# A two-layer graph network on one core: the last graph's final head gets its own finishing steps, and the validity check moves into the issue order

## The chip, the cores and the metric

One Trainium2 chip, one of its cores. The metric is the device time of one run in microseconds, the median of three runs. Before the change it is 1749.58 us (1746.99 to 1750.99).

## The reference

Sixteen graphs of 1024 nodes with 256 features each, and a 1024 x 1024 integer adjacency that is symmetric, holds 0 or 1 and has ones on its diagonal. Two layers follow each other, each with a residual and a layer norm.

```python
# layer 0: gated sum over neighbours
e0 = leaky(einsum('bid,bjd->bij', h * a0[:, 0], h))     # e1..e3 for adj == 2, 3, 4
alpha = sigmoid(where(adj == 1, e0, neg_inf))
x = layernorm(x + einsum('bij,bjd->bid', alpha, h) + bias)
# layer 1: attention, H = 4 heads of F = 64
Wh = (X @ W).reshape(B, N, H, F)
e = leaky_relu(e_src[:, :, None, :] + e_dst[:, None, :, :], 0.2)
alpha = softmax(where(A > 0, e, -1e9), axis=2)
x = layernorm(x + elu(einsum('bijh,bjhf->bihf', alpha, Wh)).reshape(B, N, H * F))
```

## The kernel before

Everything of a graph stays on the core: its nodes are 8 row blocks of 128 (`NB`), which form two halves of four blocks (`NH`, `NQ`); a half has two *pairs* of blocks. The function `stages` builds some 60 named generators for a graph, each a list of steps with `yield` between them. A table gives every step a due time: `FIRST` for graph 0, `LAST` for graph 15, `TIMES` for the 14 between, with 112 of table time between graphs. `issue` (before: L1136 and on) sorts all steps of all graphs by due time and emits them. The tables thus set nothing but the order of instructions on each engine; an engine takes its instructions in that order and waits for its inputs at each of them. Steps of neighbouring graphs lie between each other: while one graph does its attention, the next does its gates. The last graph has no next one, so its attention runs alone at the end.

What the stages near the end of a graph do, for each of the four heads `h` and the two halves:

- `pos` (VectorE, L646): for one head, one half and one of 8 source blocks, the masked comparison that tells on which side of the leaky slope an edge lies; 128x512. 64 of them in a graph.
- `acc` (TensorE, L658): the product of that mask with the head's factors; it needs the `pos` tile. `acc_low` (ScalarE, L673) and `acc_sum` (VectorE, L681) add its two halves of precision into `u`, 128x2x130 for one head of one pair.
- `weigh`: for the second half first `ts - u` on VectorE (L758, 128x520 for four heads), then a product with `rho` (`times`, L746), which in the last two graphs is eight ScalarE instructions of 128x65, one for each of 2 rows and 4 heads.
- `divide`: VectorE adds the two parts (L768, 128x512), forms the denominator (L771) and its reciprocal (L773), and `times` multiplies by it (eight ScalarE instructions of 128x64).
- `elu` (ScalarE Exp, L793, 128x512) and `join` (two VectorE instructions, L785 and L787, 128x512) give the activation and add it to the residual `y`.
- `moments1`, `gathered1` (VectorE, L432 and L438), `spread1` (GpSimd, L456 and L457), `shift1` (VectorE, L465) and `norm1` (L475 on VectorE, L477 on ScalarE) are the layer norm; `leave` (L802) sends the rows out, for the last half in two transfers, and its last step takes the running maximum of the reciprocals (`zinv`, L804).

All of `weigh`, `divide`, `elu` and `join` handle a pair with all four heads at once, so for the second half they can begin only when the last head's `acc` has been summed.

The fast path holds only for adjacencies of zeros and ones that are symmetric and for scores of bounded size. After `issue` comes a check of the whole batch (L1316 to L1337): the sums of adjacency and mask (`more`, through a TensorE product `pmore`), the largest score (`span`), the largest reciprocal (`zinv`), three comparisons, a transpose on TensorE (`pm`), a minimum (`good`) and `flag`. This part lies outside the order written out by hand; the framework's own scheduler placed it, and its early pieces stand earlier in the stream. Then every engine loads `flag` (L1339) and branches over a general path that isn't taken here (L1342).

At the start of the kernel, `setup` loads small weights through SyncE's queue and multiplies them on VectorE (L237, L239); `turn`, `mask` and `cast` bring the adjacency in, `score`, `leak`, `leaky`, `sigmoid`, `below`, `lower`, `upper`, `self_loop` make the gate, `agg` sums over the neighbours.

Of the kernel before, what the change touches and what calls it, by code (L numbers as in the profile page):

```python
# [27 lines left out]
P = 128  # L28
# [168 lines left out]
def stages(nc, k, pl, b, xg, adjg, outg, sums, span, zinv):  # L197
# [516 lines left out]
    def parts(half, pair):  # L714

        u = t["u", half, pair]
        return u[..., 0:F], u[..., F : 2 * F], u[..., 2 * F], u[..., 2 * F + 1]

    def second(half, pair):

        return t["u", half, pair][..., F : 2 * F + 1]

# [18 lines left out]
    def times(val, by):  # L741

        if late:
            for q in range(2):
                for h in range(H):
                    nc.scalar.activation(  # L746
                        val[:, q, h, :], val[:, q, h, :], AF.Copy, scale=by[:, q, h : h + 1]
                    )
        else:
            by = by.unsqueeze(3).to_broadcast(list(val.shape))  # L750
            nc.vector.tensor_tensor(val, val, by, ALU.mult)

    def weigh():
        for half, pair in PAIRS:
            ib = half * NQ + 2 * pair
            u2 = second(half, pair)
            if half:
                nc.vector.tensor_tensor(u2, t["ts", pair][..., 0 : F + 1], u2, ALU.subtract)  # L758
                yield
            times(u2, t["rho"][:, ib : ib + 2])  # L760
            yield

    def divide():
        t["rz"] = small("rzs", NB, H)
        for half, pair in PAIRS:
            ib = half * NQ + 2 * pair
            o, u2, z2, z1 = parts(half, pair)
            nc.vector.tensor_tensor(o, o, u2, ALU.add)  # L768
            yield
            rz = t["rz"][:, ib : ib + 2]  # L770
# [8 lines left out]
    def join():  # L779
        for half, pair in PAIRS:  # L780
            o, ex, _, _ = parts(half, pair)
            yp = t["y", half][:, 2 * pair : 2 * pair + 2, :].rearrange(
                "p q (h f) -> p q h f", h=H
            )
            nc.vector.scalar_tensor_tensor(o, o, 0.0, yp, ALU.max, ALU.add)  # L785
            yield
            nc.vector.scalar_tensor_tensor(yp, ex, 1.0, o, ALU.min, ALU.add)  # L787
            yield

    def elu():  # L790
        for half, pair in PAIRS:
            o, ex, _, _ = parts(half, pair)
            nc.scalar.activation(ex, o, AF.Exp)  # L793
            yield

    def leave():
        for half in range(NH):
# [5 lines left out]
            if half == NH - 1:  # L803
                nc.vector.tensor_tensor(zinv, zinv, t["rz"], ALU.max)  # L804
            yield

# [11 lines left out]
        weigh=weigh(), divide=divide(), elu=elu(), join=join(),  # L818
        moments1=moments("1"), gathered1=gathered("1"),
        spread1=spread("1"), shift1=shift("1"), norm1=norm("1"), leave=leave(),  # L820
    )

# [104 lines left out]
    "leave": [206.44, 240.93],  # L927
}
FIRST = {
    "aload": [-145.70, -145.40, -144.40, -143.60, -141.20, -140.10],  # L930
    "cast": [-146.10, -145.60, -144.60, -143.90, -142.60, -142.00, -140.90, -139.50],
    "turn": [-145.90, -145.10, -144.50, -143.20, -142.30, -141.30, -140.30, -139.30],
    "mask": [-145.30, -144.90, -143.80, -142.80, -141.70, -141.10, -139.40, -139.10],
    "setup": [-142.90, -140.70, -138.30],
    "xt": [-147.20, -147.10, -147.00, -146.80],
    "xtc": [-146.90, -146.70, -146.60, -146.40],
    "xta": [-146.50, -145.80, -144.20, -142.20, -141.80, -139.90, -139.60, -137.00],
    "score": [
        -146.20, -145.50, -144.80, -144.70, -143.40, -143.10, -142.10, -141.50, -140.40,
        -138.90, -138.60, -136.60,  # L940
    ],
    "leak": [
        -145.20, -144.30, -144.10, -144.00, -143.00, -142.70, -141.60, -141.40, -139.70,
        -138.50, -137.70, -136.40,
    ],
    "leaky": [
        -145.00, -143.70, -143.50, -143.30, -142.40, -141.90, -141.00, -140.60, -139.20,
        -137.90, -137.30, -135.60,
    ],
    "sigmoid": [-142.50, -140.80, -138.20, -137.10, -136.10, -135.00, -133.50, -132.80],  # L950
    "below": [
        -140.50, -140.20, -138.80, -138.00, -137.50, -136.80, -135.70, -135.20, -134.30,
        -132.70,
    ],
    "lower": [
        -140.00, -139.80, -138.40, -136.70, -136.00, -135.90, -134.90, -134.70, -133.40,
        -131.90,
    ],
    "upper": [-139.00, -137.60, -136.50, -135.10, -134.20, -133.00, -132.30, -131.80],
    "self_loop": [-138.70, -137.40, -135.50, -134.60, -133.80, -132.50, -131.60, -131.20],  # L960
    "agg": [
        -138.10, -137.80, -137.20, -136.20, -135.30, -134.80, -134.50, -133.90, -133.60,
        -133.20, -132.60, -132.40, -132.10, -131.40, -131.30, -130.60,
    ],
    "residual": [-136.90, -134.40, -133.70, -133.30, -133.10, -132.00, -130.90, -130.20],
    "moments0": [-135.80, -134.10, -132.90, -132.20, -131.10, -130.70, -130.40, -130.10],
    "gathered0": [-135.40, -134.00, -131.70, -131.50, -130.50, -130.30, -96.07, 17.17],
    "spread0": [-131.00, 20.28],
    "shift0": [-130.80, 24.26],
    "norm0": [6.67, 11.00, 11.41, 12.51, 25.36, 25.99, 26.71, 27.01],  # L970
    "yt": [17.15, 19.47, 29.04, 29.13],
    "ytc": [19.36, 19.69, 29.17, 29.53],
    "project": [20.27, 22.38, 25.24, 26.22, 32.78, 40.85, 41.12, 41.80],
    "wh": [25.15, 27.94, 28.22, 36.80, 41.06, 42.84, 42.85, 44.25],
    "sources": [43.57, 44.67],
    "rows": [44.50, 47.17],
    "keep_rows": [46.30, 54.62],
    "top_dve": [46.04, 47.34, 49.10, 49.48, 50.03],
    "top_pe": [46.11, 49.26],
    "exps": [51.13],  # L980
    "product": [51.24, 51.61, 51.65, 55.99, 64.09, 71.97, 73.66, 74.28],
    "high": [54.44, 56.34, 58.73, 61.00, 69.95, 72.79, 74.04, 74.66],
    "low": [54.68, 57.50, 65.30, 66.50, 71.75, 77.68, 77.72, 77.72],
    "sload": [50.22, 76.32, 79.88, 84.60, 99.79, 115.99, 126.87, 141.84],
    "pos": [
        56.38, 56.65, 59.61, 60.83, 61.90, 62.47, 66.98, 72.25, 78.79, 79.58, 80.30,
        81.29, 81.91, 83.89, 85.64, 86.24, 94.25, 94.83, 97.97, 99.15, 100.99, 101.36,
        101.95, 101.97, 105.63, 106.23, 106.73, 107.47, 108.82, 109.31, 109.42, 109.44,
        111.05, 111.90, 112.37, 114.78, 114.79, 114.81, 115.82, 117.22, 117.23, 120.53,
        122.14, 122.30, 123.00, 123.69, 124.94, 127.40, 128.22, 130.84, 132.75, 133.15,  # L990
        134.26, 137.15, 140.15, 141.06, 143.44, 144.05, 145.63, 146.94, 153.65, 154.27,
        155.46, 159.89,
    ],
    "acc": [
        61.10, 61.65, 61.72, 63.59, 69.81, 72.90, 74.47, 75.10, 81.40, 83.30, 83.92,
        84.50, 84.62, 86.15, 88.72, 89.34, 98.53, 98.69, 100.90, 100.97, 102.11, 102.79,
        105.80, 106.18, 108.03, 108.18, 108.25, 109.02, 109.72, 109.72, 110.35, 110.44,
        113.56, 114.38, 116.31, 117.04, 117.43, 119.10, 119.20, 119.89, 122.26, 122.73,
        122.79, 124.03, 124.41, 124.82, 125.15, 127.73, 134.85, 139.77, 140.29, 142.76,
# [388 lines left out]
```

## Time and profile before

| | before |
|---|---|
| median of three runs | 1749.58 us |
| profiled execution, its own time | 1748.92 us |
| its span in the trace | 1747.1 us |
| TensorE busy | 1695.6 us (97%) |
| VectorE busy | 1639.0 us (94%) |
| ScalarE busy | 1237.6 us (71%) |
| granted TensorE clock | 0.99 |

Between 120 and 1550 us TensorE is busy for 1429.49 of 1430.00 us. The stretches that matter here are the first 120 us and those from 1550 us on. ScalarE's two activation tables, one with Sigmoid and one with Exp, replace each other: 87 table loads of 1283 ns on the fast path.

### The profile page before, as it was taken

The page shows a single profiled execution, that of the slowest core. Times are in us where ns is not written, and L with a number is a line of the kernel's source. Part 1 is how long each engine was busy: PE and PEld are TensorE (multiplying, and loading weights), DVE is VectorE, ACT ScalarE, POOL GpSimd, SP SyncE. Part 2 cuts the span into 40 slices and gives each one's busy share as a digit, 9 for nine tenths or more (in the row PEclk, how much of TensorE's full clock was granted, in tenths as well). Part 3 has the DMA queues.
Part 4 walks back from the last instruction along what each step waited for, and adds up shares of the span by engine and source line. Part 5 has one row for each costly group of instructions (what it writes and reads, how often), then busy time and mean ns, then how long its engine had stood idle before and what let it go on. Part 6 is the DMA issues. An engine that isn't in the chain of part 4 may idle for free.

```text
span 1747.1 us, 29629 instructions
## 1 busy us (share of the span) xinstructions
PE 1695.6 (97%) x10579; PEld 1494.8 (86%) x10579; DVE 1639.0 (94%) x3640; ACT 1237.6 (71%) x2770; POOL 107.1 (6%) x138
## 2 busy tenths in 40 slices
PE   7999999999999999999999999999999999999884
PEld 4789898998979889898998989889898998979883
DVE  4498999999999999999999999999999999999997
ACT  6673967759587685967759586685957769585675
POOL 0001000010000101000010000101000010000100
PEclk9999999999999999999999999999999999999987
DMA  5452343434334343343434334343342435331020
GB/s 184 109 127 75 93 109 88 109 91 129 90 90 101 109 119 91 98 98 91 109 93 135 81 98 108 99 115 91 97 110 78 109 74 139 79 74 49 26 67 26
DMA packets 249274, 168.60 MB, mean 97 GB/s; under 512 B 133280, under 2 KB 232736, under 8 KB 249120
## 3 DMA queue, kind: packets, MB, share of 16 engines
q1 hardware_dynamic: 249120, 166.63, 36.3%
q8 instruction: 86, 1.41, 0.3%
q14 instruction: 68, 0.56, 0.1%
HBM read 118.10 MB, written 17.04 MB: 77 GB/s over the span
## 4 chain that ended last, share of the span: by engine, by line
PE 83%; issue 7%; DVE 4%; ACT 3%; DMA 1%; POOL 0%; SPq 0%; POOLq 0%; ACTq 0%; DVEq 0%
PE agg L415 24%; PE acc L658 24%; PE tot L701 13%; PE e L344 11%; PE pw L505 6%; PE pg L383 2%; DVE pos L646 1%; PE pt L308 1%; PE pt L486 1%; DMA sbc<-sdram 1%; DMA aT<-a 0%; ACT mT L295 0%; ACT a L273 0%; DVE gm L628 0%; DVE gate L364 0%
## 5 line engine op out<-in xcount | busy, mean ns | idle before, releaser
L646 DVE SCALAR_TENSOR_TENSOR pos<-sbc,nd,mT 128x512 fp32r<-128x512 f32 x1024 | 732.0, 738 | 7.6 <-DMA sbc<-sdram 4.5
L658 PE MATMUL acc<-gm,pos 128*128 128x260 f32 x4096 | 613.3, 293 | 6.5 <-DVE u L681 2.8
L658 PEld LDWEIGHTS acc<-gm,pos 128*128 128x128 f32 x4096 | 538.7, 190 | 19.5 <-issue 3.8
L415 PE MATMUL agg<-xb,gate 128*128 128x256 f32 x2048 | 463.3, 379 | 0.0
L415 PEld LDWEIGHTS agg<-xb,gate 128*128 128x128 f32 x2048 | 380.0, 190 | 46.9 <-DVE gate L407 0.6
L701 PE MATMUL tot<-gm,allm 128*128 128x264 f32 x2048 | 328.4, 297 | 7.1 <-ACT gm L621 5.0
L701 PEld LDWEIGHTS tot<-gm,allm 128*128 128x128 f32 x2048 | 281.1, 190 | 11.7 <-ACT gm L621 5.2
L344 PE MATMUL e<-xT,xTa 128*128 128x512 f32 (+3 forms) x768 | 265.6, 490 | 3.1 <-ACT xTa L332 1.6
L344 PEld LDWEIGHTS e<-xT,xTa 128*128 128x128 f32 x768 | 135.3, 191 | 106.9 <-issue 53.4
L673 ACT COPY low<-acc 128x260 f32<-128x260 f32 x256 | 89.9, 377 | 190.3 <-PE acc L658 190.3
L693 ACT CAST allm<-mT 128x512 fp32r<-128x512 uint8 x256 | 157.5, 616 | 27.9 <-PE tot L701 26.6
L477 ACT ACTIVATE y<-y,shift,rstd 128x256 f32<-128x256 f32 x254 | 136.8, 591 | 41.8 <-DVE shift L465 41.8
L273 ACT ACTIVATE a<-a 128x1024 bf16<-128x1024 int32 x128 | 135.6, 1060 | 41.0 <-DMA aT<-a 19.3
L295 ACT ACTIVATE mT<-aT 128x1024 uint8<-128x1024 bf16 x120 | 127.2, 1060 | 6.4 <-DMA aT<-a 6.3
L456 POOL TENSOR_SCALAR std<-mv 128x4 f32<-128x4 f32 x64 | 27.0, 421 | 1626.0 <-DVE mv L438 1426.5
L364 DVE TENSOR_TENSOR gate<-e,gate 128x512 f32<-128x512 f32 x192 | 104.2, 550 | 21.3 <-ACT gate L356 21.2
L505 PE MATMUL pw<-w_aug,yT 128*128 128x264 f32 x512 | 122.2, 387 | 0.7 <-ACT yT L495 0.6
L681 DVE TENSOR_TENSOR u<-acc,low 128x260 f32<-128x260 f32 x256 | 102.1, 419 | 16.6 <-ACT low L673 16.6
L432 DVE BATCH_NORM_STATS2 st<-y 128x6 f32<-128x256 f32 x256 | 105.8, 415 | 1.2
L505 PEld LDWEIGHTS pw<-w_aug,yT 128*128 128x128 f32 x512 | 93.4, 190 | 15.6 <-ACT yT L495 1.7
L356 ACT ACTIVATE gate<-e 128x512 f32<-128x512 f32 x192 | 90.0, 486 | 14.6 <-PE e L344 14.5
L400 DVE TENSOR_TENSOR gate<-gate,mT 128x1024 f32<-128x1024 f32 (+7 forms) x128 | 95.8, 748 | 4.5 <-PE pg L383 2.4
(97 smaller groups left out, 1775.9 us busy)
## 6 DMA issues: line engine op xcount, KB each, us to landing
a<-in_adj_dram SPq DMA_DIRECT2D x128, 512.0 KB, 4.7
sbc<-sdram SPq DMA_DIRECT2D x128, 256.0 KB, 4.6
out_dram<-y SPq DMA_DIRECT2D x31, 512.0 KB, 3.5
xb<-in_x_dram SPq DMA_DIRECT2D x15, 1024.0 KB, 5.2
aT<-a SPq DMA_TRANSPOSE x120, 3.1
xb<-in_x_dram SPq DMA_DIRECT2D x2, 512.0 KB, 4.2
sdram<-srow SPq DMA_DIRECT2D x32, 8.0 KB, 1.4
out_dram<-y SPq DMA_DIRECT2D x2, 256.0 KB, 2.3
```

Source lines behind the costliest of these rows:

```text
L273: nc.scalar.activation(t["a16", ib], t["a32", ib], AF.Copy, accum_out=sums[:, 0, at : at + 1])
L295: nc.scalar.activation(t["mT"][:, :, ib * P : (ib + 1) * P], t["aT", ib], AF.Square, accum_out=sums[:, 1, at : at + 1],)
L344: nc.tensor.matmul(e[:, 0:n], lhsT=t["xTa", jb][:, c, :], rhs=t["xT"][:, c, at : at + n], start=(c == 0), stop=(c == DC - 1),)
L364: nc.vector.tensor_tensor(ge, t["e", jb, at][:, 0:n], ge, ALU.max)
L415: nc.tensor.matmul(agg[:, 0:D], lhsT=t["gate"][:, jb, ib * P : (ib + 1) * P], rhs=t["xb"][:, jb, :], start=(jb == 0), stop=(jb == NB - 1),)
L432: nc.vector.bn_stats(st, t["y", half][:, q, :])
L477: nc.scalar.activation(y, y, AF.Identity, bias=shift, scale=rstd)
L505: nc.tensor.matmul(pw[:, 0:WD], lhsT=t["yT"][:, c, jb * P : (jb + 1) * P], rhs=k.w_aug[:, c, :], start=(c == 0), stop=(c == DC - 1),)
L646: nc.vector.scalar_tensor_tensor(p_, t["sbc", half, h], t["nd"][:, jb, h : h + 1], t["mT"][:, jb, half * HALF : (half + 1) * HALF], ALU.is ...
L658: nc.tensor.matmul(t["acc", half, h, q // 2][:, q % 2, 0 : 2 * E], lhsT=t["pos", half, h, jb][:, q * P : (q + 1) * P], rhs=pl.gm[:, h, jb] ...
L693: nc.scalar.copy(m_, t["mT"][:, j0 : j0 + 4, ib * P : (ib + 1) * P])
L701: nc.tensor.matmul(tot[:, 0 : H * F1], lhsT=t["allm", ib, jb // 4 * 4][:, jb % 4, :], rhs=pl.gm[:, :, jb, l, F:E], start=(jb == 0 and l == 0),
```

## The change

Parts of it:

1. In the last graph's second half, `weigh`, `divide`, `elu` and `join` handle heads 0 to 2 only (`heads`); instructions on all heads become narrower (128x390, 128x384), ScalarE's eight products become six, and each of the two `join` instructions becomes two, one for each row.
2. Head 3 gets stages of its own: `weigh_end`, `divide_end`, `elu_end`, `join_end`. Their products are on VectorE. In other graphs these stages issue nothing.
3. The check becomes the stage `verdict` in seven steps, in the issue order of the last graph. In the other graphs it issues only the maximum `zinv`, which was in `leave`.
4. `FIRST` and `LAST` are new throughout; `TIMES` keeps all its rows and gets five new ones for the new stages.

```diff
+    def heads(half):
+        return slice(0, H - 1 if last and half else H)
...
             if half:
-                nc.vector.tensor_tensor(u2, t["ts", pair][..., 0 : F + 1], u2, ALU.subtract)
+                ts = t["ts", pair][:, :, hs, 0 : F + 1]
+                nc.vector.tensor_tensor(u2, ts, u2, ALU.subtract)
                 yield
-            times(u2, t["rho"][:, ib : ib + 2])
+            times(u2, t["rho"][:, ib : ib + 2, hs])
...
-            nc.vector.scalar_tensor_tensor(o, o, 0.0, yp, ALU.max, ALU.add)
-            yield
-            nc.vector.scalar_tensor_tensor(yp, ex, 1.0, o, ALU.min, ALU.add)
+            rows = (0, 1) if last and half else (slice(0, 2),)
+            for q in rows:
+                nc.vector.scalar_tensor_tensor(o[:, q], o[:, q], 0.0, yp[:, q], ALU.max, ALU.add)
+            yield
+            for q in rows:
+                nc.vector.scalar_tensor_tensor(yp[:, q], ex[:, q], 1.0, o[:, q], ALU.min, ALU.add)
...
+    END = [(H - 1, pair) for pair in range(NQ // 2)]
+    def weigh_end():
+        for h, pair in END:
+            if last:
+                u2 = second(1, pair)[:, :, h]
+                nc.vector.tensor_tensor(u2, t["ts", pair][:, :, h, 0 : F + 1], u2, ALU.subtract)
+            yield
+    def divide_end():
+        for h, pair in END:
...
+            rho, rz = (t[name][:, ib : ib + 2, h] for name in ("rho", "rz"))
+            o, u2, z2, z1 = parts(1, pair, h)
+            nc.vector.tensor_tensor(z2, z2, rho, ALU.mult)
+            for q in range(2):
+                nc.vector.scalar_tensor_tensor(
+                    o[:, q], u2[:, q], rho[:, q : q + 1], o[:, q], ALU.mult, ALU.add
+                )
+            yield
+            nc.vector.scalar_tensor_tensor(rz, z1, Z_MIN, z2, ALU.max, ALU.add)
+            yield
+            nc.vector.reciprocal(rz, rz)
+            yield
+            for q in range(2):
+                nc.vector.tensor_scalar(o[:, q], o[:, q], rz[:, q : q + 1], None, ALU.mult)
+            yield
+    def elu_end():
+        for h, pair in END:
+            if last:
+                o, ex, _, _ = parts(1, pair, h)
+                nc.scalar.activation(ex, o, AF.Exp)
+            yield
+    def join_end():
...
+            yp = nodes(1, pair)[:, :, h]
+            nc.vector.scalar_tensor_tensor(o, o, 0.0, yp, ALU.max, ALU.add)
+            yield
+            nc.vector.scalar_tensor_tensor(yp, ex, 1.0, o, ALU.min, ALU.add)
             yield
...
+    def verdict():
+        if last:
...
+            nc.vector.tensor_reduce(more, sums, AX.X, ALU.add)
+            nc.vector.tensor_tensor(more[:, 0:1], more[:, 1:2], more[:, 0:1], ALU.subtract)
+            nc.vector.tensor_scalar(span[:, 1], span[:, 1], -1.0, None, ALU.mult)
+            nc.vector.tensor_reduce(
+                worst[:, 1:2], span.rearrange("p s b h -> p (s b h)"), AX.X, ALU.max
+            )
+        yield
...
+            nc.vector.tensor_copy(worst[:, 0:1], pmore[:, 0:1])
+        yield
+        nc.vector.tensor_tensor(zinv, zinv, t["rz"], ALU.max)
+        yield
+        if last:
+            nc.vector.tensor_reduce(
+                worst[:, 2:3], zinv.rearrange("p b h -> p (b h)"), AX.X, ALU.max
+            )
+            for i, limit in enumerate((0.5, SPAN_MAX, ZINV_MAX)):
+                nc.vector.tensor_scalar(
+                    bad[:, i : i + 1], worst[:, i : i + 1], limit, None, ALU.is_le
+                )
+            nc.vector.tensor_reduce(bad[:, 3:4], bad[:, 0:3], AX.X, ALU.min)
+        yield
...
+            nc.tensor.transpose(pm[0:1, 0:P], bad[:, 3:4], k.ident)
+        yield
+        if last:
+            nc.vector.tensor_reduce(good, pm[0:1, 0:P], AX.X, ALU.min)
+            nc.vector.tensor_scalar(k.flag, good, 0.0, None, ALU.is_equal)
+        yield
...
-            if half == NH - 1:
-                nc.vector.tensor_tensor(zinv, zinv, t["rz"], ALU.max)
```

The order of steps of the last graph that the two tables give, from the last `pos` on (a number is the step within its stage):

```
before: pos[63] acc[62] moments1[0] acc[63] divide[7] acc_low[14] acc_sum[14] acc_low[15]
  elu[1] weigh[2] join[2] gathered1[0] weigh[3] acc_sum[15] weigh[4] divide[8] weigh[5]
  divide[9] join[3] divide[10..14] elu[2] divide[15] moments1[1] elu[3] ... join[4] spread1[0]
  join[5] moments1[4] ... join[6] join[7] norm1[0] ... moments1[7] ... gathered1[7]
  spread1[1] shift1[1] norm1[3] leave[0] norm1[4..7] leave[1]
after:  pos[63] acc[60..63] weigh[2] divide[7] acc_low[14] moments1[0] acc_sum[14] acc_low[15]
  acc_sum[15] elu[1] weigh[3] weigh_end[0] join[2] weigh[4] gathered1[0] weigh[5] join[3]
  divide[8] divide[9] moments1[1] moments1[2] divide[10] ... elu[2] divide[12] divide[13]
  divide_end[0] divide_end[1] moments1[3] divide[14] divide_end[2] verdict[0] divide[15]
  divide_end[3] join[4] join[5] verdict[1] ... elu_end[0] join_end[0] weigh_end[1] verdict[2]
  join_end[1] spread1[0] divide_end[4] divide_end[5] moments1[4] ... elu[3] ... verdict[3]
  divide_end[7] elu_end[1] gathered1[5] join[6] verdict[4] join_end[2] verdict[5] shift1[0]
  join[7] join_end[3] verdict[6] moments1[6] norm1[0] moments1[7] ... gathered1[7] leave[0]
  spread1[1] shift1[1] norm1[4..7] leave[1]
```

In graph 0 the new order puts `setup`'s first transfers and its products on VectorE earlier (the products between `leaky[5]` and `leaky[6]`), `below[3]` and `below[4]` ahead of `agg[0]`, and `score[11]` ahead of `agg[1]`. In the last graph `sigmoid[6]` now lies between two Exp instructions of graph 13, and ScalarE's stream holds 89 table loads on the fast path.

## The prediction

> **What bounds the kernel now.** I read the busy times by stretch first. From 120 to 1550 us TensorE is full, so order there changes nothing; it can matter before 120 us and in the tail, where the last graph runs alone. The columns are TensorE's products, its weight loads, VectorE, ScalarE and GpSimd, each busy us and instructions, then clock and DMA.
>
> ```profile
> 20.00:40.00 20.00, 15.49 (x91) 9.73 (x89) 12.08 (x30) 18.95 (x35) 0.00 (x0) 1.00 0.74 243
> 1610.00:1630.00 20.00, 20.00 (x134) 18.89 (x133) 19.21 (x54) 14.95 (x40) 2.53 (x4) 1.00 0.15 41
> 1650.00:1670.00 20.00, 10.64 (x63) 9.41 (x61) 19.34 (x47) 17.52 (x64) 0.00 (x0) 0.83 0.17 52
> 1710.00:1720.00 10.00, 7.23 (x42) 6.57 (x42) 8.63 (x17) 3.85 (x13) 0.00 (x0) 0.83 0.01 2
> 1720.00:1730.00 10.00, 4.64 (x31) 3.77 (x30) 8.71 (x21) 7.12 (x28) 0.00 (x0) 0.90 0.00 0
> 1730.00:1740.00 10.00, 0.00 (x0) 0.00 (x0) 7.95 (x26) 7.78 (x25) 2.86 (x4) 0.50 0.15 52
> ```
>
> From 1650 us on the full engine is VectorE, not TensorE. Next I read the timeline of the tail: start, us, engine, line, count.
>
> ```profile
> 1721.77 2.07 DVE L646 SCALAR_TENSOR_TENSOR pos<-sbc,nd,mT 128x512 fp32r<-128x512 f32 x3
> 1725.36 0.70 DVE L758 TENSOR_TENSOR u<-ts,u 128x520 f32<-128x520 f32 x1
> 1725.98 0.69 DVE L785 SCALAR_TENSOR_TENSOR u<-u,y 128x512 f32<-128x512 f32 x1
> 1726.09 3.94 ACT L746 ACTIVATE u<-u,rho 128x65 f32<-128x65 f32 x16 [0.42 <-DVE u L758]
> 1729.94 2.00 ACT L746 ACTIVATE u<-u,rzs 128x64 f32<-128x64 f32 x8
> 1732.51 2.01 ACT L746 ACTIVATE u<-u,rzs 128x64 f32<-128x64 f32 x8
> 1735.09 2.06 ACT L477 ACTIVATE y<-y,shift,rstd 128x256 f32<-128x256 f32 x4
> 1737.34 0.30 DVE L438 BATCH_NORM_AGGREGATE mv<-st 128x2 f32<-128x6 f32 x2
> 1739.30 1.09 ACT L477 ACTIVATE y<-y,shift,rstd 128x256 f32<-128x256 f32 x2 [2.16 <-DVE shift L465]
> 1740.17 0.19 DVE L1328 TENSOR_REDUCE worst<-zinv 128x1 f32<-128x32 f32 x1
> 1741.52 0.14 DVE L1337 TENSOR_SCALAR flag<-good 1x1 int32<-1x1 f32 x1
> ```
>
> The last `pos` ends at 1723.84, the last statistic at 1737.64: a stretch S of 13.80 us. ScalarE runs in it without a gap from 1726.09 to 1737.15, VectorE waits for it in turns. After S come 2.75 us to the last ScalarE norm (1740.39), the check until 1741.66, then a last group of instructions at the branch (minimum, median and maximum ns; start us):
>
> ```profile
> L1342 ACTq COMPARE_BRANCH  x1: 50/50/50, 1742.4 to 1742.4; - x1
> L1342 PEldq COMPARE_BRANCH  x1: 3498/3498/3498, 1742.5 to 1742.5; - x1
> L1342 ACTq EVENT_SEMAPHORE  x1: 17/17/17, 1745.4 to 1745.4; - x1
> L1342 DVEq EVENT_SEMAPHORE  x1: 21/21/21, 1745.7 to 1745.7; - x1
> L1342 PEldq EVENT_SEMAPHORE  x1: 51/51/51, 1746.0 to 1746.0; - x1
> ```
>
> Every engine loads the flag at 1741.7, branches, and goes on 3 to 3.5 us later, TensorE last; the span ends 1.1 us after that.
>
> **The change, part by part: the split head.** The new order does not put the three heads' work ahead of the last head's: `weigh[2]` stands behind `pos[63]`. So the stage that counts is S again, and I add up VectorE's work in it. The step from one start to the next is 0.60 us for 512 elements (1725.98 to 1726.58) and 0.35 for 260 (two L681 in 0.77, one in 0.42), that is 0.07 fixed and 1.03 ns for an element; by it 384 and 390 take 0.47, 192 0.27, 128 and 130 0.20, 64 0.14. A statistic of 256 takes 0.34, an aggregate or a denominator 0.08, a reciprocal 0.10.
>
> Before, 35 instructions: sums 0.70, two of 520 1.24, additions 1.20, six joins 3.60, denominators and reciprocals 0.36, statistics 2.72 and 0.64, a shift 0.08, two pieces of the check 0.15, in all 10.7. The other 3.1 of S are waits, mostly for ScalarE.
>
> After, 70 instructions: sums 0.70, three-head subtractions 0.94, additions 0.94 and eight joins of 192 2.16, the first half's two joins 1.20, the end head's 0.40 + 0.16 + 0.56 + 0.56 + 0.80 = 2.48 (subtractions, `z2` times `rho`, products and sums, divisions, joins), denominators and reciprocals 0.72, statistics, aggregates and shift 3.44. That is 12.6. The check adds 13 instructions: 0.40 + 0.15 + 0.17 + 0.28 + 0.14 + 0.18 + 0.19 + 0.45 + 0.16 + 0.28 + 0.14 = 2.5 by full durations, 1.5 by steps. So 14.1 with no wait at all and 15.1 with the check's pieces, each of which reads the one before, at full length. ScalarE's list in S is 24 products at 0.247 (5.9), two Exp of 384 at 0.41, two of 128 at 0.15 and the first half's Exp 0.54: 7.6 (the rows' steps are 0.247 for a product, 0.54 for 512 elements from 1731.97 on; the narrower ones are estimates from it at about 1 ns for an element). It no longer fills S; VectorE does. I take S = 15.1, nearest to the sum; the ceiling is every one of 70 instructions waiting for the one before (0.10 longer each): 21.1.
>
> **The check.** Behind the last ScalarE norm 1.27 us disappear (1740.39 to 1741.66). TensorE's last work is then `pm`, so it can load the flag and branch while VectorE still works, and its 1746.0 leaves the path; ScalarE's 1745.4 remains: another 0.6. For the tail: +1.3 (S), -1.3, -0.6, so **-0.6 us**, from -1.6 (S 14.1) to +5.4 (S 21.1). SyncE's three last transfers keep their order, the output lands (2.3 us) before the branch is done.
>
> Two pages speak to these terms and nothing above needs them. The Trainium skill, "VectorE: DVE Perf Modes", section on the TRN2 errata, says that each Vector instruction pays a fixed cost and that small tiles pay it each time; it also gives a measured 151 cycles, about 0.157 us. The rows' 0.07 is smaller for instructions that don't wait for each other. An estimate by the page's 151 cycles is 14.1 + 70 x 0.087 = 20.2 for S, which would make the change slower. The Trainium skill, "Advanced Engine Details and Errata", Control Flow Timing, gives a compare-and-branch about 108 ns; the row has 3498 on TensorE. By the page no engine's branch would be longer than another's and the 0.6 would be nothing.
>
> **Pieces of the check that leave earlier places.** L1324, L1325 and one L1331 (0.17 + 0.28 + 0.15 = 0.6) leave 1650.9 to 1652.5, where VectorE is near its limit (4.41 of 5.00): -0.6 to 0, I take -0.3. Those at 1591.5 and 1592.6 leave a stretch where TensorE is full: 0.
>
> **The new order before the last `pos`.** VectorE's work is the same, so only its idle time can go or come: 0.66 + 1.02 + 0.46 + 0.30 + 1.37, 3.8 us from 1650 us on. A new order can remove it or add as much: -3.8 to +3.8, and I take 0, because the critical runs (`top_dve`, `product`, `low`, `pos`) keep their sequence. The two further table loads are 2 x 1.283 = 2.6 us of ScalarE, hidden behind TensorE's full stretch (row 1610 to 1630, ScalarE 14.95 of 20); uncovered they would cost 2.6.
>
> **The start.** `setup`'s eight VectorE instructions fill 30.81 to 34.0 us; earlier they fall into VectorE's wait of 5.12 us ahead of 30.20. Their three transfers (0.43 us of issue each) go ahead of two adjacency loads, 1.3 us at most for these. `below[3]` and `below[4]` ahead of `agg[0]`: `below[4]` needs the third sigmoid, which ended at 38.60, plus 0.6 for its transposes, against 38.45 when `agg[0]` began: up to +0.8. ScalarE is busy 18.95 of 20 us there, so little can be gained: I take -0.5, from -3 (TensorE's idle after its first start) to +2.1.
>
> The step `zinv` in the other graphs is the same 0.18 us instruction a little earlier: 0. The empty stages issue nothing.
>
> **Sum.** -0.6 - 0.3 + 0 - 0.5 = -1.4. Against the profiled execution's 1748.92 this is 1747.5; that execution lies 0.66 below the median, so 1748.2 on the median's scale.
>
> **The rivals.**
> - *A, forecast:* VectorE takes ScalarE's place as the bound of the tail, and nothing measurable changes: 1748.2. For it: 3.4 us of new work against 3.1 us of waits. Chance 0.40.
> - *B, faster:* S at its floor (tail -1.6), half of the idle time before it gone (-1.9), the check's pieces -0.6, the start -1.5: -5.6, 1744.0. For it: two whole tables are new and VectorE has 3.8 us of idle time to lose. Against: the engine is nearly full. 0.31.
> - *C, slower:* in S most small instructions read what the one before wrote, and wait it out. At the ceiling of 21.1 the tail costs +5.4, less 0.8 for the rest: +4.6, 1754.2. It decides from S = 20.0. For it: pairs of the end head's instructions are chained; against: statistics and other heads lie between them. With a worse start included, 0.16.
> - *D, the split does nothing:* S stays 13.8, only the check's move counts: -1.9 - 0.3 - 0.5 = -2.7, 1746.9. 0.13.
>
> **How the numbers follow.** About 0.2%, 3.5 us, is what a measurement of this kernel can tell from no change. A and D lie within it (0.53), B is faster (0.31), C slower (0.16). The range goes from below B to near C, 1743.0 to 1753.5; A's own is 1745 to 1751.
>
> **What would show it.** In the profile after: S near 15 us with VectorE at over 90% and ScalarE with gaps in it; `flag` written before the last statistics; TensorE's branch over before ScalarE's and the span's end about 5 us behind the last norm; some 89 table loads; TensorE idle as much as before up to 40 us. I'd be wrong if the last `pos` ended more than 3 us off its old distance from the start, or if S stayed under 13.

## The result and the profile after

| | before | after |
|---|---|---|
| median of 20 runs each, in turns | 1749.42 us (1746.80 to 1753.22) | 1746.63 us (1742.96 to 1749.88) |
| profiled execution, its own time | 1748.92 us | 1749.88 us |
| its span in the trace | 1747.1 us | 1747.9 us |
| VectorE busy | 1639.0 us | 1639.5 us |
| ScalarE busy | 1237.6 us | 1240.0 us |
| S, last `pos` to last statistic | 13.80 us | 14.89 us |
| end of S to the span's end | 9.46 us | 8.29 us |

The ratio after to before is 0.9985, its 95% interval 0.9979 to 0.9991: 2.8 us faster, within the 0.2% called no change, yet clear of zero. The profiled execution of after is the slowest of its twenty, so the spans must not be compared; stretches of the two traces can be.

The busy times by stretch of after, with the same columns as those of before:

```profile
20.00:40.00 20.00, 16.12 (x99) 10.04 (x98) 13.35 (x33) 19.24 (x36) 0.00 (x0) 1.00 0.66 213
1650.00:1670.00 20.00, 11.23 (x67) 9.70 (x65) 18.82 (x42) 16.47 (x61) 1.27 (x2) 0.83 0.10 31
...
1720.00:1730.00 10.00, 5.14 (x32) 4.24 (x32) 9.75 (x26) 6.39 (x25) 0.00 (x0) 0.94 0.00 0
1730.00:1740.00 10.00, 0.96 (x3) 0.58 (x3) 9.47 (x55) 6.31 (x20) 1.65 (x3) 0.50 0.00 0
```

From 1720 us on VectorE went from 8.71 and 7.95 of 10 us to 9.75 and 9.47, ScalarE from 7.12 and 7.78 to 6.39 and 6.31. Within S itself ScalarE was busy for 12.17 of 13.80 us before and is for 10.41 of 14.89 after, VectorE for 11.96 and 14.50: the bound of the tail has changed engines. In 20 to 40 us TensorE does 0.63 us more than before.

The timeline of after's tail, VectorE's and ScalarE's lines (start, us, engine, line, count, idle time before):

```profile
1722.03 2.69 DVE L646 SCALAR_TENSOR_TENSOR pos<-sbc,nd,mT 128x512 fp32r<-128x512 f32 x4
...
1724.63 0.56 DVE L768 TENSOR_TENSOR u<-ts,u 128x390 f32<-128x390 f32 x1
...
1726.44 2.98 ACT L755 ACTIVATE u<-u,rho 128x65 f32<-128x65 f32 x12
...
1729.82 1.54 ACT L755 ACTIVATE u<-u,rzs 128x64 f32<-128x64 f32 x6 [0.40 <-DVE rzs L783]
...
1731.29 0.40 DVE L873 TENSOR_REDUCE more<-sums 128x2 f32<-128x256 f32 x1
...
1736.32 0.31 ACT L843 ACTIVATE u<-u 128x128 f32<-128x128 f32 x1 [2.36 <-DVE u L836]
...
1736.90 0.26 DVE L897 TENSOR_SCALAR bad<-worst 128x1 f32<-128x1 f32 x3
...
1738.59 0.14 DVE L908 TENSOR_SCALAR flag<-good 1x1 int32<-1x1 f32 x1
1738.66 0.73 DVE L432 BATCH_NORM_STATS2 st<-y 128x6 f32<-128x256 f32 x2
1739.32 0.29 DVE L438 BATCH_NORM_AGGREGATE mv<-st 128x2 f32<-128x6 f32 x2
...
1741.28 1.09 ACT L477 ACTIVATE y<-y,shift,rstd 128x256 f32<-128x256 f32 x2 [1.54 <-DVE shift L465]
```

ScalarE now has gaps (0.40 us for VectorE's reciprocal, 2.36 us for its division), VectorE has hardly any. The check (L873 to L908) lies within S, and `flag` is written at 1738.59 to 1738.73, ahead of the last statistics. The last `pos` ends at 1724.72, the last aggregate at 1739.61, the last norm at 1742.37.

The last group of instructions of after, at the branch (minimum, median and maximum ns; start us):

```profile
L1442 SPq EVENT_SEMAPHORE  x8: 17/17/17, 1744.7 to 1746.2; - x8
L1442 PEldq COMPARE_BRANCH  x1: 3655/3655/3655, 1739.4 to 1739.4; - x1
L1442 PEldq EVENT_SEMAPHORE  x1: 51/51/51, 1743.1 to 1743.1; - x1
L1442 ACTq EVENT_SEMAPHORE  x1: 17/17/17, 1745.0 to 1745.0; - x1
L1442 DVEq EVENT_SEMAPHORE  x1: 21/21/21, 1745.8 to 1745.8; - x1
```

TensorE branches at 1739.4 and goes on at 1743.1, before ScalarE's 1745.0: it has left the path. But VectorE goes on at 1745.8 and SyncE's eight semaphores last until 1746.2, so the span ends 5.5 us behind the last norm (before 6.7).

Outside the tail one thing stands out that I had not read in before's trace. Timeline of before, SyncE's transfers and VectorE's wait:

```profile
1556.95 11.35 SPq L288 DMA_TRANSPOSE aT<-a  x2
1568.40 2.27 SPq L636 DMA_DIRECT2D sbc<-sdram  x2
...
1573.24 0.75 DVE L646 SCALAR_TENSOR_TENSOR pos<-sbc,nd,mT 128x512 fp32r<-128x512 f32 x1 [2.05 <-DMA sbc<-sdram]
```

and of after, SyncE:

```profile
1566.73 0.37 SPq L636 DMA_DIRECT2D sbc<-sdram  x1
1571.64 1.24 SPq L288 DMA_TRANSPOSE aT<-a  x1
```

Before, a row load for `pos` (L636) stood in SyncE's queue behind two transposes of graph 15's adjacency (L288); the second waited for its `cast`, so the load started at 1568.40 and VectorE waited 2.05 us for it. After, the load goes out at 1566.73, ahead of the transpose, and the wait is gone. The busy times show that TensorE waited too, first before, then after:

```profile
1570.00:1590.00 20.00, 18.71 (x123) 17.18 (x122) 17.68 (x34) 15.28 (x33) 0.00 (x0) 1.00 0.42 113
```

```profile
1570.00:1590.00 20.00, 20.00 (x142) 19.14 (x141) 19.26 (x35) 17.91 (x38) 0.00 (x0) 1.00 0.43 107
```

### The profile page after: what moved, and what is told of

Its sections match the earlier page's. It is cut to its first block, busy times and chain, and to the rows that moved or that the text cites. A ratio compares the mean times of both kernels' runs of the same rounds, so it can differ in the third digit from the quotient of the medians.

```text
span 1747.9 us, 29657 instructions
## 1 busy us (share of the span) xinstructions
PE 1697.7 (97%) x10579; PEld 1494.4 (85%) x10579; DVE 1639.5 (94%) x3664; ACT 1240.0 (71%) x2766; POOL 106.8 (6%) x138
## 5 line engine op out<-in xcount | busy, mean ns | idle before, releaser
L356 ACT ACTIVATE gate<-e 128x512 f32<-128x512 f32 x192 | 90.1, 487 | 11.3 <-PE e L344 11.3
```

## The experiments

Three places were left as the origin of the 2.8 us, and each is a theory: *Start* (the new `FIRST`), *Queue* (that transfer), *Tail* (the split and the check). The first four kernels take them apart. Each was timed against the kernel before on its own chip, eleven runs each unless said otherwise. The kernels e1 to e7 and a2 ran on one chip, w1 and w2 on a second, w3 and w4 on a third.

**The new tables without the new start** (e1_old_first): after, with all rows of the old `FIRST`; the rows of the new stages stand at its end. One row of each kind, against after:

```diff
 FIRST
-    "setup": [-140.4, -137.2, -133.3],
+    "setup": [-142.9, -140.7, -138.3],
...
-    "verdict": [245.29, 252.29, 264.28, 276.27, 330.86, 365.10, 497.34],
+    "verdict": [245.72, 245.72, 245.72, 245.72, 245.72, 245.72, 245.72],
```

> The changed kernel with graph 0's old order (the table FIRST of before, the rows of the new stages at its end). Three theories. Queue: the 2.8 us come from the new order where graphs 14 and 15 overlap, so this keeps them: 1746.6 us, -2.8 against before, and the start up to the first 150 us differs from the changed kernel by less than 1 us. Tail: they come from the split head and the moved check, so this keeps them too: -2.8. Start: they come from graph 0's new order, so nothing is left: 0.

Measured: ratio 1.0001 [0.9992, 1.0010] (the brackets hold the 95% interval), no gain is left. Start expects that.

**The old order up to the last `pos`, the new tail** (e2_old_order_new_tail): after, with the old `FIRST`; in `LAST` the steps up to `pos[63]` have their old times, those behind it follow in the new order. One row of `LAST`, whose last four steps lie behind `pos[63]`, against the kernel before:

```diff
-    "weigh": [5123.18, 5683.12, 6000.69, 6014.21, 6025.75, 6056.50],
+    "weigh": [5123.18, 5683.12, 5850.93, 5854.93, 5856.43, 5857.43],
```

> Both old orders up to the last pos, then the changed kernel's tail: the split head and the check as a stage. Queue: no gain, within 0.8 us of before; the stretch from the last pos to the end of the span stays 23.2 us. Tail: -2.8 us against before. Start: 0.

Measured: 1.0007 [0.9997, 1.0016]. S is 14.9 as in after, and nothing is gained: Tail falls.

**The new order up to the last `pos`, the old tail** (e3_new_order_old_tail): the kernel before, with after's due times up to `pos[63]` and the old order behind it. The same row:

```diff
-    "weigh": [5123.18, 5683.12, 6000.69, 6014.21, 6025.75, 6056.50],
+    "weigh": [4872.46, 5401.61, 5575.51, 5577.01, 5578.01, 5579.01],
```

> The kernel before with the new order of the last graph up to the last pos and nothing else new: old graph 0, all heads finished together, the check behind the issue order. Queue: -2.5 us against before, gained between 1540 and 1610 us. Tail: 0. Start: 0.

Measured: 1.0007 [0.9998, 1.0016]. The 2.5 us that Queue expected (ratio 0.9986) lie outside: by the times this order alone gains nothing.

**One due time in the kernel before** (e4_turn_behind_sload), which puts one transpose behind one row load in SyncE's queue and moves nothing on the other engines.

```diff
-    "turn": [-112.19, -102.61, -90.43, -73.16, -61.35, -41.19, -35.31, -25.39],
+    "turn": [-112.19, -102.61, -90.43, -73.16, -61.35, -41.19, -32.00, -25.39],
```

> The kernel before with a single step moved: the last graph's seventh transpose (turn[6]) is issued behind graph 14's second row load (sload[1]) on SyncE's queue instead of ahead of it; every other engine's stream is the same. Queue: the row load no longer waits for the cast that the transpose waits for, VectorE's wait of 2.05 us near 1573 us goes, and -2 us against before; at least -1. Tail and start: 0.

Measured: 0.9994 [0.9984, 1.0004]: the interval, from 2.8 us faster to 0.7 slower, holds both 2 us and nothing. The timeline of this kernel, SyncE:

```profile
1557.24 1.23 SPq L288 DMA_TRANSPOSE aT<-a  x1
...
1565.06 0.38 SPq L636 DMA_DIRECT2D sbc<-sdram  x1
1567.34 1.23 SPq L288 DMA_TRANSPOSE aT<-a  x1
```

The load goes at 1565.06, ahead of the waiting transpose; VectorE's wait of 2.05 us is not in this trace. So the stall goes, and no gain of time is shown, as in e3, where the queue is mended too. The next four kernels test Start directly and take the tail apart.

**The changed kernel once more** (a2_after_again), for a second profile; no edit.

> The changed kernel once more, for a second profile and a second ratio. All theories: time against before -2.8 us (ratio 0.9985, its first interval 0.9979 to 0.9991). By profile, relative to before's execution: the stretch from the start of the 881st to the 929th `pos` (about 1522 to 1607 us) -2.0 to -2.9 again; the last `pos` to the last aggregate (S) 14.9 within 0.3; the last `pos` to the span's end 23.2 within 1. The start (65th `pos`) may lie anywhere from -1.2 to +1.2, since four kernels with the same start spread so far.

Measured: 0.9990 [0.9981, 0.9999]; S 14.9 again, last `pos` to the end 24.1 counted from its start (after 23.9).

**The new start alone** (e5_new_first): the kernel before, with all rows of after's `FIRST` but those of the new stages.

```diff
-    "setup": [-142.9, -140.7, -138.3],
+    "setup": [-140.4, -137.2, -133.3],
...
```

> The kernel before with the new FIRST alone: only the start's order differs. Theory Start (the gain is made in the first 120 us): -2.8 us, ratio 0.9984. Theories Queue (the transfer queue at 1568 us) and Tail: 0, ratio 1.000. By profile: the stretch 1522 to 1607 us as in before (excess of 0.8 to 2.9 kept), the tail as in before.

Measured: 0.9991 [0.9982, 1.0000]. Between the theories: by the ratio the start gives some 1.6 us, with an interval from 0 to 3.1, so neither nothing nor the whole gain is excluded.

**The check in VectorE's waits** (e6_check_in_gaps): after, with six of its seven steps moved.

```diff
-    "verdict": [5941.96, 5975.61, 6027.35, 6055.62, 6085.49, 6138.78, 6170.81],
+    "verdict": [5464.391, 5464.392, 5486.801, 6055.62, 6488.67, 6488.68, 6488.69],
```

> The changed kernel with six of the seven steps of the check (all but the fourth, the transposed product's reading kept in order) moved to where VectorE waits anyway: the first two behind pos[58], where VectorE waits 1.25 us for a copy, the third behind acc_sum[13], the last three behind spread1[1], in the 1.47 us in which VectorE waits for GpSimd. Theory VectorE bounds the tail (my forecast): S goes from 14.9 to 13.1, and the flag is still written before the last ScalarE norm ends; the run is 1.7 us below the changed kernel. Rival, VectorE's instructions in S wait for each other, so that the check's pieces lay in their gaps: S stays 14.5 to 14.9, time as the changed kernel.

**No split** (e7_no_split): after, with all four heads together; the stages of the last head issue nothing, `weigh[2]` and `weigh[4]` wait for the last head's sums, and the check stays a stage.

```diff
     def heads(half):
-        return slice(0, H - 1 if last and half else H)
+        return slice(0, H)
...
-            rows = (0, 1) if last and half else (slice(0, 2),)
+            rows = (slice(0, 2),)
...
-    "weigh": [4872.46, 5401.61, 5594.10, 5696.51, 5721.09, 5781.75],
+    "weigh": [4872.46, 5401.61, 5634.37, 5696.51, 5669.97, 5781.75],
```

> The changed kernel without the split: the second half's weigh, divide, elu and join again on all four heads, no stages for the last head; the check stays a stage in steps. Theory VectorE takes ScalarE's place (my forecast): the split moves about 2 us of work from ScalarE to VectorE and gains nothing: S within 0.7 of 14.9, time within 0.7 us of the changed kernel. Rival, the split pays by itself and the check costs it: S 16 or more, time +1.5 or more against the changed kernel.

Measured: e6 0.9987 [0.9978, 0.9996], e7 0.9989 [0.9981, 0.9998]; the times tell neither from the changed kernel. The timelines do. Last `pos` and last aggregate on VectorE, first of e6, then of e7:

```profile
1717.95 2.69 DVE L646 SCALAR_TENSOR_TENSOR pos<-sbc,nd,mT 128x512 fp32r<-128x512 f32 x4
...
1734.27 0.30 DVE L438 BATCH_NORM_AGGREGATE mv<-st 128x2 f32<-128x6 f32 x2
```

```profile
1717.64 2.69 DVE L646 SCALAR_TENSOR_TENSOR pos<-sbc,nd,mT 128x512 fp32r<-128x512 f32 x4
...
1736.15 0.29 DVE L438 BATCH_NORM_AGGREGATE mv<-st 128x2 f32<-128x6 f32 x2
```

S is 1734.57 - 1720.64 = 13.9 in e6 and 1736.44 - 1720.33 = 16.1 in e7. Without the split the check costs S 16.1 - 13.8 = 2.3 us (the prediction had 2.5); with it 14.9 - 13.9 = 1.0. With the check out of the way, split and unsplit tails are alike (13.9 and 13.8). So the split by itself gains nothing. Where the difference of 2.3 and 1.0 comes from, VectorE's busy time in S tells: 11.96 of 13.80 us in before, 12.89 of 16.11 in e7, 13.17 of 13.93 in e6, 14.50 of 14.89 in after. Without the split the check adds 0.9 us of work and 1.4 us of waiting; with it 1.3 us of work, and 0.4 us of waits are filled. So the split saves the check most of its waiting and hides little of its work. Of e7's two theories the rival came nearer in S; its 1.5 us of time were not seen (0.8 us on the means, against all 31 runs of the changed kernel).

**Why one kernel's runs differ.** By now eight kernels lay apart by no more than the scatter of one (standard deviation 1.9 us in the kernel before). For every kernel the table has the start of the 65th `pos` (relative to before's execution, 190.90 us), the time gained from the 897th to the 929th (about 1550 to 1607 us) and from there to the 993rd (1694 us), the stretch from the start of the last `pos` to the span's end, how long the first four scores took, and whether TensorE's granted clock was halved for 3.4 us at 81 to 88 us:

| kernel | `FIRST` | 65th | 897 to 929 | 929 to 993 | to the end | first scores | half clock |
|---|---|---|---|---|---|---|---|
| before | old | 0 | 0 | 0 | 24.0 | 3.75 | no |
| e3 | old | -0.2 | -1.7 | +0.7 | 24.7 | 3.75 | no |
| e1 | old | -1.2 | -2.3 | +1.0 | 24.8 | 1.95 | yes |
| e4 | old | -0.6 | -1.8 | +0.3 | 24.4 | 2.39 | yes |
| e2 | old | +1.1 | -0.4 | -0.6 | 24.8 | 1.96 | yes, and at 29 to 33 us |
| after | new | -0.1 | -2.1 | +0.7 | 23.9 | 3.75 | yes |
| e5 | new | -0.3 | -0.4 | -0.7 | 24.6 | 3.75 | yes |
| e7 | new | -1.6 | -2.1 | +1.3 | 25.1 | 3.51 | no |
| a2 | new | -2.4 | -2.3 | +1.1 | 24.1 | 1.96 | yes |
| e6 | new | -3.3 | -2.3 | +1.0 | 23.8 | 2.75 | no |

Rows with the same two last columns can be compared: no and 3.75 or 3.51 us, -0.1 (mean of before and e3) and -1.6; yes and about 2 us, -0.9 (e1 and e4) and -2.4. Both pairs give the new `FIRST` 1.5 us; other pairs, with the first scores' time taken off, reach from 0.6 (e1 and after) to 2.3 (before and e6). So the last two columns set much of the scatter in the 65th. The column 929 to 993 goes with the clock too: between 1650 and 1695 us it was halved for 10.2 us in e2 and e5, for 13.7 in before, e3 and after, for 17.1 in e1, e4, a2 and e6, for 20.5 in e7. The same happens in the tail. TensorE's clock in before by single microseconds (columns as above, the last but two is the clock):

```profile
1714.00:1715.00 1.00, 1.00 (x8) 1.00 (x8) 1.00 (x3) 0.73 (x3) 0.00 (x0) 0.65 0.06 16
1715.00:1716.00 1.00, 1.00 (x6) 1.00 (x6) 1.00 (x2) 0.34 (x2) 0.00 (x0) 0.50 0.00 0
1716.00:1717.00 1.00, 1.00 (x6) 1.00 (x6) 0.98 (x3) 0.00 (x0) 0.00 (x0) 0.50 0.00 0
1717.00:1718.00 1.00, 1.00 (x8) 1.00 (x7) 0.65 (x1) 0.00 (x0) 0.00 (x0) 0.64 0.00 0
```

The timeline of TensorE there, first of before, then of e4 with the same instructions:

```profile
1712.42 0.51 PE L658 MATMUL acc<-gm,pos 128*128 128x260 f32 x2 [1.59 <-DVE u L681]
1713.36 5.39 PE L658 MATMUL acc<-gm,pos 128*128 128x260 f32 x30 [0.43 <-DVE u L681]
```

```profile
1711.15 0.51 PE L658 MATMUL acc<-gm,pos 128*128 128x260 f32 x2 [1.59 <-DVE u L681]
1712.09 3.85 PE L658 MATMUL acc<-gm,pos 128*128 128x260 f32 x30 [0.43 <-DVE u L681]
```

Thirty products of the same kind take 5.39 us in one run and 3.85 in the other; in before VectorE then waits 1.35 us for the copy behind them, in e4 it doesn't. Over all 68 runs of the kernel before in the first two groups of experiments, the mean time falls with the mean granted clock of the run: 1750.7 us at 0.988 (18 runs), 1749.4 at 0.989 (20), 1748.0 at 0.990 (28), with one run each at 0.987 and 0.991. One half-clock stretch of 3.4 us is 0.001 of the mean clock (1.7 / 1747), and goes with 1.3 us.

**Keeping TensorE busy in its gaps.** If that is the cause, work that nobody needs, put where TensorE waits, takes the scatter away, and some time with it. Forty transposes of the identity went into four gaps, first in the changed kernel (w1_after_warm) and in the kernel before (w2_before_warm). Nobody reads what they write.

```diff
+    def warm(place, n):
+        for _ in range(n):
+            nc.tensor.transpose(place[:, 0:P], k.ident, k.ident)
...
                 pt = t["xt", c, half] = quads("pt")
+                if first and c + half < 2 and c == 0:
+                    if half == 0:
+                        k.warm = pl.ps_u.tile([P, 2, HALF], F32, tag="u", name="warm")[:, 0]
+                    warm(k.warm, 1 if half else 11)
...
         for jb, at, n in PIECES:
+            if first and (jb, at) == (0, 0):
+                warm(k.warm, 2)
+            if b == 1 and (jb, at) == (0, 0):
+                warm(k.warm, 10)
...
+            if last and half and h == 2:
+                k.warm = bank("warm")
             for jb in range(NB):
                 for q in range(NQ):
+                    if last and half and h > 1 and jb == 0 and q % 2 == 0:
+                        warm(k.warm, {(2, 0): 9, (2, 2): 2, (3, 0): 5, (3, 2): 0}[h, q])
```

> The changed kernel with 40 idle transposes of the identity added on TensorE, whose output nobody reads, in four gaps: 11 ahead of the first product (2 to 4.4 us), 3 more until the first score, 10 ahead of graph 1's first score (81 to 83 us), 16 at the last two heads' starts (1712 to 1720 us). Theory Clock (the runs of one kernel differ because TensorE is sometimes granted half its clock for 3.3 us after an idle stretch): the first scores take 0.49 us a product in every run instead of 0.94 in some (1.8 us in about half of the runs), no half clock at 83 us (1.2 to 1.6 us in about 6 of 10) and none at 1714 us (1.3 us in 7 of 10): 2.6 us below the changed kernel on the mean, ratio to before 0.9972, and the spread of its runs is smaller than 1.3 us (standard deviation; before 1.9). Rival, the added products only lengthen TensorE's queue, and the half clock comes elsewhere: as the changed kernel, 0.9987, or slower.

> The kernel before with the same 40 idle transposes. Theory Clock: 2.6 us below the kernel before, ratio 0.9985, a smaller spread. With this noise out of the way the distance between this run and the changed kernel with the same transposes is the change's own: theories Start and Queue together 2.2 us (1.5 for the new FIRST, as pairs of profiles with the same clock show it, and 0.7 for the transfer queue at 1568 us); theory Tail alone 0.

Measured: w1 1743.38 us (five runs, 1741.80 to 1744.30), ratio 0.9963 [0.9950, 0.9977]; w2 1747.03, ratio 0.9985 [0.9976, 0.9994]. The theory's 0.9972 and 0.9985 hold; the rival falls. The standard deviation of a run is 1.1 us in w1, 0.8 in w2. The timeline of TensorE in w2 (L226 are the added transposes, L356 the scores):

```profile
1.46 2.61 PE L226 MATMUL warm<-ident 128*128 128x128 f32 x11 [1.46 <-POOL ident masks.py:199]
...
9.82 1.96 PE L356 MATMUL e<-xT,xTa 128*128 128x512 f32 x4 [0.88 <-DVE xTa L338]
...
81.32 6.71 PE L356 MATMUL e<-xT,xTa 128*128 128x512 f32 x16 [0.50 <-ACT xTa L340]
...
1710.53 1.14 PE L226 MATMUL warm<-ident 128*128 128x128 f32 x9
...
1713.22 3.87 PE L674 MATMUL acc<-gm,pos 128*128 128x260 f32 x30 [0.21 <-DVE u L697]
```

The first four scores take 1.96 us, the thirty products of the tail 3.87, and the clock column shows no half clock in w1 or w2 up to 120 us nor between 1680 and 1720 us. The half clock between 1650 and 1680 us stays (13.7 and 17.1 us of it).

With the noise lower, the rest could be measured. **The new start alone, with the transposes** (w3_new_first_warm), and **the check in the waits, with the transposes** (w4_check_in_gaps_warm); the edits are those of e5 and e6.

> The kernel before with the new FIRST alone and the 40 idle transposes. The changed kernel and the kernel before, both with these transposes, lie 3.4 us apart on their means (1743.2 and 1746.6). Theory Start: 1.9 us of it are made before 191 us (the 65th `pos` starts at -3.95 against -2.00 relative to before's execution), so this kernel's mean is 1744.7; the stretch 1550 to 1607 us stays as in the kernel before. Theory Queue (all of it is made behind 1550 us): 1746.6.

> The changed kernel with the check's steps in VectorE's waits and with the 40 idle transposes: the best of what the runs have shown. S was 13.9 us with the check there, 14.9 without that move: 1.0 us below the changed kernel with the transposes, mean 1742.2, ratio to before 0.9959. Rival: what VectorE gains there it waits for at the branch, where the engines fetch their next instructions: 1743.2, ratio 0.9965.

Measured: w3 0.9972 [0.9963, 0.9981], its mean 1744.87 (ten runs) against 1746.63 of w2 (eleven): the new start is worth 1.8 us (standard error 0.35; expected 1.9). The two ran on different chips; each against its own chip's kernel before, they lie 2.1 us apart (standard error 0.7). The 65th `pos` is at -4.1 in w3, -4.0 in w1, -3.9 in w4, against -2.0 in w2. Start is shown. w4: 0.9971 [0.9961, 0.9982], mean 1744.71 (eight runs), neither the expected 1742.2 nor the rival's 1743.2, though its trace has S at 13.9. VectorE's lines ahead of the last `pos` in w4 say where that microsecond went:

```profile
1709.75 3.39 DVE L658 SCALAR_TENSOR_TENSOR pos<-sbc,nd,mT 128x512 fp32r<-128x512 f32 x5
1713.07 0.41 DVE L889 TENSOR_REDUCE more<-sums 128x2 f32<-128x256 f32 x1
```

In after VectorE waited 1.25 us behind these five `pos`, for the copy that the next `acc_sum` reads, and e6 put four instructions of the check there. With the clock full the wait is gone: in w1 `acc_sum` follows the `pos` at once, in w4 it begins only at 1714.01, behind the four. From the 993rd to the last `pos` w4 takes 28.7 us and w1 27.8; S is 0.9 us shorter in w4, and the two cancel. Whether w4 or w1 is the better kernel stays open: their intervals overlap, and they ran on different chips. Both beat the kernel before.

The busy times by stretch at the start, first of w2 (old start), then of w3 (new start):

```profile
0.00:20.00 20.00, 16.88 (x74) 10.88 (x75) 6.59 (x16) 10.31 (x19) 1.26 (x10) 1.00 0.54 184
20.00:40.00 20.00, 15.51 (x93) 10.63 (x92) 12.07 (x29) 16.96 (x32) 0.00 (x0) 1.00 0.69 218
...
80.00:120.00 40.00, 38.79 (x218) 30.05 (x217) 38.17 (x71) 34.02 (x81) 0.00 (x0) 1.00 0.47 121
```

```profile
0.00:20.00 20.00, 17.29 (x74) 11.10 (x75) 7.07 (x18) 10.34 (x19) 1.27 (x10) 1.00 0.63 202
20.00:40.00 20.00, 16.20 (x101) 10.96 (x100) 13.82 (x32) 17.76 (x35) 0.00 (x0) 1.00 0.63 200
...
80.00:120.00 40.00, 39.33 (x217) 30.78 (x216) 38.69 (x71) 36.01 (x84) 0.00 (x0) 1.00 0.47 131
```

TensorE does 0.41, 0.69 and 0.54 us more in these three stretches, 1.6 in all. TensorE's longest wait between 25 and 40 us, first of w2, then of w3:

```profile
32.29 0.55 PE L395 MATMUL pg<-ident,gate 128*128 128x128 f32 x3 [0.91 <-DVE gate L376]
```

```profile
27.92 2.43 PE L356 MATMUL e<-xT,xTa 128*128 128x128 f32 x8 [0.59 <-DVE gate L376]
```

In w2 `setup`'s eight products fill VectorE from 28.82 to 32.04, and the `gate` that TensorE waits for comes behind them; in w3 they stand at 22.59 to 25.82, where VectorE would have waited. Over 20 to 40 us TensorE's waits for VectorE's `gate` fall from 1.5 to 1.0 us, those for ScalarE's `mT` from 0.7 to none, and those for its `a` rise from 2.3 to 2.6.

## Why the prediction was right, and where it was not

The time, 1748.2 us predicted and 1746.6 measured, was 1.6 us off. The sum was -1.4 and the gain is 2.8 (a second measurement, a2, has 1.8): the time lies in the range, but its largest part came from a term that I had put too low, and the tail has the other sign. Term by term:

- *S = 15.1*: 14.85 to 14.89 in the five traces with the new tail (after, a2, e1, e2, w1). That VectorE takes ScalarE's place, over 90% busy and with gaps on ScalarE, is what the windows show. That the sum came out so near is partly luck. Its 12.6 us without the check were too few: with twelve of the check's thirteen instructions elsewhere S is still 13.9 (e6). The check's 2.5 were too many: they cost 1.0. The 3.1 us of waits before were too large as well: VectorE is idle for 1.84 us of S before and for 0.39 after. And the two rows that I used give 0.99 ns for an element and 0.09 us fixed, not 1.03 and 0.07; the steps of 64 elements took 0.16 to 0.20 us, not 0.14. The ceiling of 21.1, rival C, is far off. By the estimate from the Trainium skill, "VectorE: DVE Perf Modes", section on the TRN2 errata, S would have been 20.2; the measurement, 14.89, decides for the smaller fixed cost of the rows.
- *The check, 2.5 of work in S*: it costs S 2.3 without the split (e7) and 1.0 with it (e6).
- *-1.3 and -0.6 behind S*: only -0.8 on the mean of the traces (8.9 us from the last aggregate's end to the span's with the new tail, in after, a2, e1, e2 and w1; 9.7 with the old one, in before, e3, e4, e5, w2 and w3; between the two traces shown 1.2). TensorE's branch left the path as said, but VectorE goes on at 1745.8 and SyncE's semaphores last until 1746.2, so that over half of the 1.9 was not got. The tail is thus +0.2 on the mean, not -0.6. The Trainium skill's "Advanced Engine Details and Errata", Control Flow Timing, with about 108 ns for a branch, does not describe it: TensorE's took 3655 ns, and ScalarE and VectorE, whose branches took 50 and 72 ns, went on 2.9 and 3.6 us after them.
- *The check's pieces that left earlier places, -0.3*: no run takes them apart.
- *The new order before the last `pos`, 0*: not shown to be wrong, but its reason was. I counted VectorE's idle time "from 1650 us on" and left 1550 to 1650 unread but for one full window. There the 2.05 us wait for a row load stood, and TensorE stood still for 1.29 of 20 us, 0.90 of them for the `pos` that waited. The traces with the new order gain 1.8 us more between the 897th and the 929th `pos` than those with the old one, and lose 1.0 of it again by the 993rd, part of which goes with longer half clock. In time e3 shows nothing of it, and w1 and w4 have 1.7 and 0.2 us over w3 (w1 from another chip, w4 with the check moved). Its size stays open.
- *The start, -0.5*: the term that was sized worst: -1.8 (w3 against w2). I argued that ScalarE's 18.95 of 20 us left little to gain; but TensorE waited there for VectorE's `gate` too (0.91 us in w2), and with the new start TensorE is busy for 1.6 us more up to 120 us. That `setup`'s products fall into a wait of VectorE was right. The sign that TensorE would idle as much as before up to 40 us failed: in 0 to 40 us it is busy for 1.1 us more in w3 than in w2. My bounds (-3 to +2.1) held the time.
- *Two more table loads*: 89 instead of 87, as said. In after TensorE is busy for 20.00 of 20 us in every window from 1550 to 1650 us, so nothing speaks against their being hidden; no run takes them apart.

So case A named the mechanism of the tail rightly; the gain came from the start, and what is left of it, up to 1 us, has no place that the times show. Rival D had the nearest time (1746.9) by a wrong road: S did not stay at 13.8. Rival B's 1.5 us for the start was near the truth; its 1.9 for lost idle time is not shown, and its cheaper tail did not come.

## What to carry to other kernels

Read every stretch in which the bound engine is not full, not only the two that the change is about: one missing row of windows hid a 2 us wait. Before a gain of a tenth of a per cent is explained, find out what makes the runs of one kernel differ; here two profiles of the same changed kernel, 1747.9 us (after) and 1743.6 (a2), differ by more than the change. Where TensorE waits in pieces of a microsecond, a few products without a reader can be worth as much as a new order of the real ones: 2.7 us on the mean in w2, 1.9 to 2.8 for the change. A wait that is there only because the clock was halved is no place for other work: in w4 it was gone.

## What the runs showed of the hardware

TensorE's half clock comes on a grid. In before its stretches begin at 1656.28, 1669.94, 1714.30 and 1727.96 us, worked out from the clock of single microseconds: all multiples of 3.41 us apart; the first three are 6.8, 6.8 and 3.4 us long, the last holds to the end. The grid lies differently in each run: in e4 it starts a window at 1710.27, and the same gaps fall across two windows. In before the window from 1710.89 to 1714.30 had TensorE idle for 1.53 + 0.43 us and was followed by half clock; in e4 the one from 1710.27 to 1713.68, idle for 0.88 + 0.43 us, was not. So some 43% of work was too little and 62% enough. All fourteen traces agree: of the windows of the grid that began at full clock, all 45 with TensorE busy for less than 49% were followed by half clock and none of the 6886 with more than 57.5%; of the 23 between, 10 were. The Trainium skill, "TensorE: Matmul & The Clock Gate", section on what is actually happening, gives a free-running window of 3413 ns, which agrees, and names an idle window as what halves the clock; here a window that was not idle did it.

At the start the granted clock stands at 1.00 in the rows, and yet four scores took 3.75 us in before and 1.96 in a2. The column shows 1.00 there for want of a record: the first record of the clock that the trace keeps, of full clock, lies at 14.47 us in before, behind these scores (9.62 to 13.37), and at 9.47 in a2, ahead of them. In the six traces where it lies up to 10.12 us they take 1.95 to 2.06 us, in the four where it lies from 13.44 on 3.75, in the four between 2.34 to 3.51. In w4 it lies at 10.38 and they take 2.34, so the added transposes shorten the wait for full clock and do not remove it in every run.
